# Joining two blocks' exponentials before the ones product in the last group of a decoder layer's self attentions

## The chip, the cores and the metric

The kernel runs on one core of a Trainium2 chip. The core has five engines, each with its own list of instructions: TensorE (PE in the profile; its weight loads are PEld), VectorE (DVE), ScalarE (ACT), GpSimd (POOL) and SyncE (SP), which issues most DMAs. An engine takes its list strictly in order and waits for others by semaphores. The metric is the device time of one execution in microseconds (us), the median of several runs.

## The reference

One decoder layer on `x` (4, 512, 512), with a context of the same shape: x plus a self attention with projections and biases, plus a cross attention without projections, plus a feed-forward part (shared MLP and one expert matrix). 16 heads of 32 columns, all in float32. What matters here is the self attention:

```python
scores = jnp.einsum('bhqd,bhkd->bhqk', q, k) * SCALE
causal = jnp.tril(jnp.ones((Td, Td), dtype=bool))
scores = jnp.where(causal, scores, -jnp.inf)
probs = jax.nn.softmax(scores, axis=-1)
ctx = jnp.einsum('bhqk,bhkd->bhqd', probs, v)
```

## The kernel before

The four batch entries are worked one after the other. For each there is a self attention (class `Attention` with `cross=False`, named `s0` to `s3`), an output projection, a cross attention (`c0` to `c3`), and a feed-forward part whose matmuls fill gaps of the next entry.

**Tiles of an attention.** The 16 heads make four groups `g` of four heads (`HG = 4`). The 512 keys are cut into four blocks `j` of 128. By causality block `j` meets the queries from `j * 128` on, so it has 512, 384, 256 or 128 columns of queries per head. Scores are held transposed (keys on partitions, queries on columns), two heads to a tile of two PSUM banks, four heads in two tiles.

**Three steps of a unit** (`attend`, line 974). A unit is a piece or two of (group, block): for an even group `g` they are `(g,0)`, then `(g,3)` with `(g,1)`, then `(g,2)` with `(g+1,2)`, then `(g+1,0)`, then `(g+1,3)` with `(g+1,1)`. Ten units in all, numbered 0 to 9. `scores` (line 397) writes the scores into PSUM, ScalarE takes their exponentials into SBUF tiles `pt` (line 443), and GpSimd sets the part above the diagonal to zero (line 451, the *mask*). The values of a unit (`values`, line 463) follow two units later: after the scores of unit `n` come the values of unit `n-2`, and at the end those of units 8 and 9 stand behind each other.

**Values** (`shares`, line 470). For each piece, four matmuls (one for each head, each 32 columns of TensorE's array wide, side by side) multiply the exponentials with `v` into the numerators, `pv[:, 0, :]` (line 486 with `u = 0`). The denominators are sums of the exponentials over the keys, made as products with a matrix of ones. For groups 0 to 2 (`added`) VectorE first adds the blocks' exponentials into one tile `sums[g]` (`add_up`, line 551, adds at line 556), and one ones product of 512 columns per head makes the sums (`summed`, line 560, matmul at line 562). For group 3, which is not added, every piece has its own ones product beside its numerators (line 486 with `u = 1`, into `pv[:, 1, :]`), all four accumulated in PSUM.

**The end of a self attention.** The sums of group 2 go to a PSUM pair of their own, `ls`. They are issued with block 0 of group 3 (lines 511 to 513). `spread` and `inverse` (lines 570 and 580) transpose the sums on VectorE, take reciprocals and spread them; `scale` (line 575) multiplies the output of groups 0 to 2 on GpSimd; group 3 is divided on VectorE (line 525). Then `out_projection` (line 739) multiplies the four groups' outputs with `wo`, group by group, with transposes of the context and of the next input between them (lines 255 to 267).

**The cross attentions** already have a joined pair of blocks, in group 1 (`joined = 1`, except in the last): `join` (line 529) adds block 2's exponentials to the second half of block 0's on VectorE, and `joint_sums` (line 539) makes one ones product of the result, placed with block 0, first of its group.

**What sets the order.** The whole body runs under `tc.manual_schedule` for TensorE, VectorE, ScalarE and GpSimd: each engine's instructions stand in the order in which the program calls them. Semaphores follow from what reads and writes which tile. PSUM is four tiles of two banks (`pair`, line 65), which all of the kernel shares. The tiles of `join` have the tag `xin`, two buffers that also hold the next entry's input during its normalization.

Of the kernel before, what the change touches and what calls it, by code (L numbers as in the profile page):

```python
# [26 lines left out]
def decoder_layer(  # L27
# [22 lines left out]
    B, S, D = x.shape  # L50
# [3 lines left out]
    NC = D // P  # L54
# [10 lines left out]
    def pair(name):  # L65

        return ps.tile([P, 2, S], F32, tag="ps", name=name)
# [80 lines left out]
    zero = const.tile([P, 1], F32, name="zero")  # L148
# [121 lines left out]
    class Attention:  # L270
        def __init__(self, q_t, k_t, v, cross, name):
            self.q_t, self.k_t, self.v, self.cross, self.name = q_t, k_t, v, cross, name
            self.nm, self.mrow, self.pv, self.out = {}, {}, {}, None
            self.more, self.sums, self.rden, self.e = {}, {}, {}, None
            self.added = (0, 2) if cross else range(NC - 1)

            self.joined = 1 if cross and name != f"c{B - 1}" else None
            self.joint, self.zero = [], None

        def maxima(self, pieces):  # L280
# [189 lines left out]
        def shares(self, g, blocks):  # L470

            js = {j for j, *_ in blocks}
            first = js == {0} if g % 2 == 0 else js == {2}
            last = js == {2} if g % 2 == 0 else 1 in js
            if first:
                self.pv[g] = pair(f"pv_{self.name}_{g}")
            pv = self.pv[g]
            for u in range(1 if g in self.added else 2):
                if u and g == self.joined and (0 in js or 2 in js):
                    if 0 in js:  # L480
                        self.joint_sums(pv, blocks[0][2])
                    continue
                for n, (j, c, pts) in enumerate(blocks):
                    for r in range(HG):
                        h = g * HG + r
                        nc.tensor.matmul(  # L486
                            pv[r * HD : (r + 1) * HD, u, j * P :],
                            lhsT=ones if u else self.v[:, j, h * HD : (h + 1) * HD],
                            rhs=pts[r // 2][:, r % 2, c : c + S - j * P],
                            start=first,  # L490
                            stop=last and n == len(blocks) - 1,
                            skip_group_check=True,
                        )
            if self.cross:


                if (first if g == 1 else js == {0}) and g - 1 in self.added:
                    self.summed(g - 1, self.pv[g - 1])
                    self.divide(g - 1)
                elif js == {0} and g > 0:  # L500
                    self.scale(g - 1)
                if 1 in js and g == NC - 1:
                    self.scale(g - 1)
                if last and g not in self.added:
                    self.divide(g)
                    if g == NC - 1:
                        self.scale(g)
                return
            if first and g == 0:
                self.out = act.tile([P, NC, S], F32, tag="o_t", name=f"oT_{self.name}")  # L510
            if (first if g in self.added else js == {0}) and g - 1 in self.added:
                self.sum_in = pv if g in self.added else pair(f"ls_{self.name}")
                self.summed(g - 1, self.sum_in)
            if js == {0} and g - 2 in self.added:
                self.scale(g - 2)
            if 1 in js and g - 1 in self.added and g not in self.added:
                self.spread(g - 1, self.sum_in)
                self.scale(g - 1)
            if last and g in self.added:
                nc.scalar.copy(self.out[:, g, :], pv[:, 0, :])  # L520
                if g > 0:
                    self.spread(g - 1, pv)
            elif last:
                num, den = pv[:, 0, :], pv[:, 1, :]
                nc.vector.tensor_tensor(
                    self.out[:, g, :], num, self.inverse(g, den), ALU.mult
                )
# [8 lines left out]
                )  # L536
                self.joint.append(to)

        def joint_sums(self, pv, zero):
            for n in range(2):  # L540
                for r in range(HG):
                    nc.tensor.matmul(
                        pv[r * HD : (r + 1) * HD, 1, n * S // 2 : (n + 1) * S // 2],
                        lhsT=ones,
                        rhs=(self.joint if n else zero)[r // 2][:, r % 2, : S // 2],
                        start=(n == 0),
                        stop=False,
                        skip_group_check=True,
                    )

# [582 lines left out]
```

## Time and profile before

| what | value |
|---|---|
| median of 3 runs | 802.95 us (802.95 to 803.22) |
| profiled execution | 803.28 us |
| its span, first to last instruction | 801.5 us |
| TensorE busy | 794.1 us, 99% of the span |
| VectorE, ScalarE, GpSimd busy | 566.4, 395.4, 340.0 us |
| granted TensorE clock, mean | 1.000 |
| line 486, numerators of self attentions, `pv_s` from `pt_s` and `v`, 128x256 | 385 ns each |
| line 534, joining adds of the cross attentions, 128x512 | 679 ns each |

A row of the page's groups names the line, the engine, the operation, the tile written and the tiles read, the shape, how many there were, the busy time and the mean of one, and then how long the engine sat idle before them and who ended that. A row of a timeline gives the start, the time that a run of like instructions took together, and the same names. Matmuls are pipelined and their ends are modelled, so the distance from one start to the next says more than a duration. A float32 matmul stands as two instructions in the trace, so four heads with one piece are x8. Busy shares are means over the whole span; what one edit is worth has to be read from its own stretch.

### The profile page before, as it was taken

How to read it: one execution, taken by the hardware profiler on the slowest of the kernel's cores; microseconds unless marked ns; L12 is line 12 of the kernel's file. 1: busy time of each engine (PE TensorE's matmuls, PEld its weight loads, DVE VectorE, ACT ScalarE, POOL GpSimd, SP SyncE). 2: the span in 40 equal slices, each digit the busy share in tenths (PEclk: the TensorE clock that was granted, in tenths of full speed). 3: DMA queues.
4: the chain of work that ended last, by engine and by line, in shares of the span. 5: the costliest groups of instructions: out<-in, count | busy, mean ns of one | idle time of the engine just before them, and what ended most of it. 6: DMA issues, size and time to landing. Idle time of an engine off the chain costs nothing.

```text
span 801.5 us, 13955 instructions
## 1 busy us (share of the span) xinstructions
PE 794.1 (99%) x5600; PEld 379.5 (47%) x5600; DVE 566.4 (71%) x963; ACT 395.4 (49%) x450; POOL 340.0 (42%) x523
## 2 busy tenths in 40 slices
PE   8999999999999999999999999999999999999998
PEld 7444554445444454444544445444444454444444
DVE  2478866888678854588867786688859766988512
ACT  2557426871547515666045752687056824674110
POOL 3435612664234732267233482266423653475100
PEclk9999999999999999999999999999999999999999
DMA  9700000001000000021100000000102000000101
GB/s 311 266 28 1 2 1 1 2 28 54 1 27 1 2 1 0 2 80 53 53 14 14 1 2 1 0 1 2 54 28 80 2 2 0 1 2 2 52 1 52
DMA packets 16337, 24.51 MB, mean 31 GB/s; under 512 B 2064, under 2 KB 6416, under 8 KB 16272
## 3 DMA queue, kind: packets, MB, share of 16 engines
q1 hardware_dynamic: 15552, 22.96, 8.3%
q8 instruction: 44, 0.72, 0.4%
q10 hardware_dynamic: 720, 0.66, 0.2%
q14 instruction: 21, 0.17, 0.1%
HBM read 19.42 MB, written 4.19 MB: 29 GB/s over the span
## 4 chain that ended last, share of the span: by engine, by line
PE 96%; ACT 2%; issue 1%; DVE 0%; POOL 0%; POOLq 0%
PE pm_qk L245 13%; PE pm_d L233 7%; PE pm_u L245 7%; PE pm_v L233 7%; PE pm_o L745 7%; PE pm_e L233 7%; PE pv_c L486 6%; PE pv_s L486 6%; PE sm_c L297 6%; PE sm_s L297 6%; PE sc_s L409 5%; PE sc_c L409 5%; PE sc_s L420 1%; PE sc_c L420 1%; PE pv_s L562 1%
## 5 line engine op out<-in xcount | busy, mean ns | idle before, releaser
L328 DVE TENSOR_REDUCE nm_s<-s_s 128x2 f32<-128x1024 f32 (+3 forms) x128 | 96.9, 810 | 31.0 <-POOL s_s L316 30.9
L328 DVE TENSOR_REDUCE nm_c<-s_c 128x2 f32<-128x1024 f32 (+3 forms) x128 | 95.9, 811 | 31.0 <-POOL s_c L316 31.0
L308 ACT COPY s_s<-sm_s 128x1024 f32<-128x1024 f32 x80 | 77.1, 1015 | 70.7 <-PE sm_s L297 36.4
L308 ACT COPY s_c<-sm_c 128x1024 f32<-128x1024 f32 x80 | 77.1, 1016 | 35.9 <-PE sm_c L297 16.2
L316 POOL TENSOR_SCALAR_AFFINE_SELECT s_c<-s_c 128x512 f32<-128x512 f32 (+1 forms) x80 | 44.1, 552 | 100.2 <-ACT s_c L308 100.2
L316 POOL TENSOR_SCALAR_AFFINE_SELECT s_s<-s_s 128x512 f32<-128x512 f32 (+1 forms) x80 | 44.0, 554 | 92.9 <-ACT s_s L308 92.9
L556 DVE TENSOR_TENSOR sum_s<-sum_s,pt_s 128x256 f32<-128x256 f32 (+2 forms) x72 | 60.0, 898 | 15.4 <-PE pv_s L486 15.4
L443 ACT ACTIVATE pt_c<-sc_c 128x1024 f32<-128x1024 f32 x64 | 61.7, 1031 | 18.4 <-PE sc_c L420 10.1
L233 PE MATMUL pm_d<-wdown_sb,hT 128*128 128x512 f32 x128 | 61.5, 610 | 0.0
L451 POOL TENSOR_SCALAR_AFFINE_SELECT pt_c<-pt_c 128x512 f32<-128x512 f32 (+1 forms) x64 | 52.5, 828 | 21.1 <-ACT pt_c L443 20.7
L245 PE MATMUL pm_u<-fT,wup_sb 128*128 128x512 f32 x128 | 59.3, 604 | 0.0
L443 ACT ACTIVATE pt_s<-sc_s 128x1024 f32<-128x1024 f32 x56 | 53.9, 1029 | 10.5 <-POOL pt_s L451 5.5
L233 PE MATMUL pm_v<-wv_sb,xnT 128*128 128x512 f32 x128 | 58.8, 600 | 0.0
L745 PE MATMUL pm_o<-wo_sb,oT_s 128*128 128x512 f32 x128 | 57.8, 596 | 0.0
L409 PE MATMUL sc_c<-cqT,ckT 32*128 32x384 f32 (+3 forms) x512 | 56.4, 464 | 0.9 <-ACT sum_c L443 0.9
L245 PE MATMUL pm_qk<-xnT,wk_sb 128*128 128x512 f32 x120 | 57.3, 607 | 0.0
L245 PE MATMUL pm_qk<-xnT,wq_sb 128*128 128x512 f32 x120 | 56.7, 604 | 0.0
L233 PE MATMUL pm_e<-wexp_sb,fT 128*128 128x512 f32 x120 | 56.3, 604 | 0.0
L451 POOL TENSOR_SCALAR_AFFINE_SELECT pt_s<-pt_s 128x512 f32<-128x512 f32 (+1 forms) x56 | 48.0, 867 | 16.8 <-ACT pt_s L443 16.2
L409 PE MATMUL sc_s<-qT,kT 32*128 32x128 f32 (+3 forms) x512 | 54.0, 464 | 0.9 <-ACT sum_s L443 0.9
L297 PE MATMUL sm_c<-ckT,cqT 32*128 32x512 f32 (+3 forms) x512 | 47.5, 460 | 0.0
L297 PE MATMUL sm_s<-kT,qT 32*128 32x512 f32 (+3 forms) x512 | 47.0, 461 | 0.0
(177 smaller groups left out, 1274.8 us busy)
## 6 DMA issues: line engine op xcount, KB each, us to landing
cv<-in_ctx_dram SPq DMA_DIRECT2D x16, 256.0 KB, 3.7
out_dram<-x SPq DMA_DIRECT2D x15, 256.0 KB, 2.1
xin<-in_x_dram SPq DMA_DIRECT2D x12, 256.0 KB, 2.6
x<-in_x_dram SPq DMA_DIRECT2D x12, 256.0 KB, 4.0
wv_sb<-in_wv_dram SPq DMA_DIRECT2D x1, 1024.0 KB, 8.3
wo_sb<-in_wo_dram SPq DMA_DIRECT2D x1, 1024.0 KB, 9.9
wup_sb<-in_wup_dram SPq DMA_DIRECT2D x1, 1024.0 KB, 9.9
wdown_sb<-in_wdown_dram SPq DMA_DIRECT2D x1, 1024.0 KB, 12.1
```

Of the source, the lines that this page charges most:

```text
L233: nc.tensor.matmul(pm, lhsT=lhs_t[:, c, t * P : (t + 1) * P], rhs=w[:, c, :], start=(c == 0), stop=(c == NC - 1),)
L245: nc.tensor.matmul(pm, lhsT=w[:, c, f * P : (f + 1) * P], rhs=rhs_t[:, c, :], start=(c == 0), stop=(c == NC - 1),)
L297: nc.tensor.matmul(scs[r // 2][:, r % 2, c : c + (i + 1) * P], lhsT=self.q_t[h, g, i * P : (i + 1) * P], rhs=self.k_t[h, g, : (i + 1) * P] ...
L308: nc.scalar.copy(s, scs[n])
L316: nc.gpsimd.affine_select(out=diagonal, in_=diagonal, compare_op=ALU.is_ge, fill=NEG, base=0, pattern=[[0, 2], [0, len(pieces)], [-1, P]], ...
L328: nc.vector.tensor_reduce(self.nm[g][:, i, 2 * n : 2 * n + 2], made[n][:, :, c : c + (i + 1) * P], axis=AX.X, op=ALU.max, negate=True,)
L409: nc.tensor.matmul(scs[r // 2][:, r % 2, c : c + S - j * P], lhsT=self.k_t[h, g, j * P : (j + 1) * P], rhs=self.q_t[h, g, j * P :], start= ...
L443: nc.scalar.activation(pt, scs[n], AF.Exp)
L451: nc.gpsimd.affine_select(out=diagonal, in_=diagonal, compare_op=ALU.is_ge, fill=0.0, base=0, pattern=[[0, 2], [0, len(pieces)], [1, P]], ...
L486: nc.tensor.matmul(pv[r * HD : (r + 1) * HD, u, j * P :], lhsT=ones if u else self.v[:, j, h * HD : (h + 1) * HD], rhs=pts[r // 2][:, r % ...
L556: nc.vector.tensor_tensor(to, to, pts[n][:, :, c : c + S - j * P], ALU.add)
L745: nc.tensor.matmul(pms[t // 2][:, t % 2, :], lhsT=a.out[:, c, t * P : (t + 1) * P], rhs=wo_sb[:, c, :], start=(c == 0), stop=(c == NC - 1),)
```

## The change

In the self attentions block 2 of group 3 is joined with block 0, as it is in the cross attentions' group 1, and the products are put in a new order. Three things happen.

1. `joined` becomes group 3 (`NC - 1`) for self attentions. The separate ones products of block 2 (256 columns a head) and of block 0 (512 columns) go. `attend` now calls `join` for this group: two adds on VectorE, 128x512 elements each, behind the adds of group 2's last block.
2. The ones products of group 3 are all made with its last unit, in this order: those of blocks 3 and 1 (the first of which starts the accumulation), then `joint_sums` with two runs of 256 columns a head: block 0's first half, and the joined half.
3. The sums of group 2 (`summed`, into `ls`) are issued behind the numerators of blocks 3 and 1, ahead of group 3's ones products, and no longer behind block 0's products.

So the end of TensorE's list in a self attention reads: numerators of block 2, of block 0, of blocks 3 and 1; sums of group 2; ones of blocks 3 and 1; joint ones. In the cross attentions `joint_sums` gets the flag `first`, and its order is what it was.

```diff
-            self.joined = 1 if cross and name != f"c{B - 1}" else None
+            self.joined = NC - 1 if not cross else 1 if name != f"c{B - 1}" else None
...
             for u in range(1 if g in self.added else 2):
                 if u and g == self.joined and (0 in js or 2 in js):
                     if 0 in js:
-                        self.joint_sums(pv, blocks[0][2])
+                        self.zero = blocks[0][2]
+                    if 0 in js and self.cross:
+                        self.joint_sums(pv, self.zero, first=True)
                     continue
+                joining = u and g == self.joined and not self.cross
                 for n, (j, c, pts) in enumerate(blocks):
                     for r in range(HG):
...
-                            start=first,
-                            stop=last and n == len(blocks) - 1,
+                            start=n == 0 if joining else first,
+                            stop=last and n == len(blocks) - 1 and not joining,
                             skip_group_check=True,
                         )
+                if joining:
+                    self.joint_sums(pv, self.zero, last=True)
+                elif g == self.joined and not self.cross and 1 in js:
+                    self.sum_in = pair(f"ls_{self.name}")
+                    self.summed(g - 1, self.sum_in)
...
-            if (first if g in self.added else js == {0}) and g - 1 in self.added:
-                self.sum_in = pv if g in self.added else pair(f"ls_{self.name}")
+            if first and g > 0 and g in self.added:
+                self.sum_in = pv
                 self.summed(g - 1, self.sum_in)
...
-        def joint_sums(self, pv, zero):
+        def joint_sums(self, pv, zero, first=False, last=False):
             for n in range(2):
                 for r in range(HG):
...
-                        start=(n == 0),
-                        stop=False,
+                        start=first and n == 0,
+                        stop=last and n == 1,
```

## The prediction

> **What bounds the kernel now.** I read the page first. Two of its lines say where a microsecond counts:
>
> ```profile
> span 801.5 us, 13955 instructions
> PE 794.1 (99%) x5600; PEld 379.5 (47%) x5600; DVE 566.4 (71%) x963; ACT 395.4 (49%) x450; POOL 340.0 (42%) x523
> ...
> PE 96%; ACT 2%; issue 1%; DVE 0%; POOL 0%; POOLq 0%
> ```
>
> TensorE is busy in 99% of the span and makes 96% of the chain that ended last. So whatever lengthens or shortens TensorE's own row of work, a stall included, goes into the time at full size, and what the other engines do counts only where TensorE waits for it. Next I read the timeline of TensorE at the end of the first self attention (line 486 with v: numerators; with ones, and line 562: denominators; line 745: output projection):
>
> ```profile
> 88.86 1.07 PE L486 MATMUL pv_s<-pt_s,v 128*32 128x256 f32 x16
> 89.75 0.61 PE L486 MATMUL pv_s<-pt_s,ones 128*32 128x256 f32 x8
> 90.18 1.04 PE L486 MATMUL pv_s<-pt_s,v 128*32 128x512 f32 x8
> 91.04 1.04 PE L486 MATMUL pv_s<-pt_s,ones 128*32 128x512 f32 x8
> 91.90 1.04 PE L562 MATMUL ls_s<-sum_s,ones 128*32 128x512 f32 x8
> 92.76 1.05 PE L486 MATMUL pv_s<-pt_s,v 128*32 128x128 f32 x16
> 93.62 1.05 PE L486 MATMUL pv_s<-pt_s,ones 128*32 128x128 f32 x16
> 94.60 3.70 PE L745 MATMUL pm_o<-wo_sb,oT_s 128*128 128x512 f32 x8
> ```
>
> The durations include a modelled tail, so I take prices from one start to the next. I call the eight rows N7 (block 2 of groups 2 and 3), O7 (ones on block 2), N8 and O8 (block 0), S (the sums of group 2), N9 and O9 (blocks 3 and 1), and the projection. N7 takes 0.89 us, O7 0.43, N8, O8, S and N9 0.86 each, O9 0.98 with the change to line 745. Nothing waits here. The same eight rows stand at 272.12, 469.09 and 642.88 us with the same spacing to 0.02 us, so one working serves four times.
>
> Then I read who feeds N9, in the timelines of ScalarE, GpSimd and VectorE:
>
> ```profile
> 88.88 1.94 ACT L443 ACTIVATE pt_s<-sc_s 128x1024 f32<-128x1024 f32 x2 [0.43 <-PE sc_s L420]
> ...
> 89.97 0.83 POOL L451 TENSOR_SCALAR_AFFINE_SELECT pt_s<-pt_s 128x512 f32<-128x512 f32 x1 [0.21 <-ACT pt_s L443]
> 90.88 0.96 POOL L451 TENSOR_SCALAR_AFFINE_SELECT pt_s<-pt_s 128x512 f32<-128x512 f32 x1
> ...
> 90.22 1.12 DVE L556 TENSOR_TENSOR sum_s<-sum_s,pt_s 128x512 f32<-128x512 f32 x1
> 91.33 0.72 DVE L583 STREAM_TRANSPOSE dt_s<-pv_s 128x512 f32<-128x512 f32 x1
> ```
>
> The exponentials of blocks 3 and 1 start when their scores leave TensorE and end at 90.82. GpSimd's two masks of them end at 90.80 and 91.84. N9 multiplies just these tiles, two heads from each, and it starts at 92.76: 0.92 us of slack. The slack is 0.92, 0.92 and 0.94 in the other three attentions (masks ending at 275.10, 472.07 and 645.83).
>
> **The change part by part.** Order before: N7 O7 N8 O8 S N9 O9. Order after: N7 N8 N9 S O9 J, where J is the joint product, two runs of 256 columns.
>
> *Removed and moved products.* Ones columns per head fall from 1280 to 1024 (O7 256 and O8 512 go, J brings 512). J has 16 instructions and 512 columns, as O8 and O9 have in columns: 0.86 us. The row of TensorE work becomes 0.43 us shorter per attention, 1.7 us in all. That is what the change would give if nothing waited.
>
> *N9 moves ahead.* What stood between N8 and N9, O8 and S (1.72 us), and O7 ahead of them (0.43 us) were its cover. After the change N8 runs from 89.75 to 90.61, and N9 wants to start at 90.61. Its first two heads wait for the first mask (90.80), its third for the second (91.84). TensorE works in its written order, so S, O9 and J queue behind N9 and cannot fill the gap. How soon does TensorE start after a release? At 156.58 two exponentials take 1.96 us, to 158.54, and the scores waiting for them start at 158.59: 0.05 us. So N9's third head starts at 91.89, and as its first two heads' short piece alone is done by then, which spares next to nothing of four heads side by side, N9 ends at 91.89 + 0.86 = 92.75. Then S, O9 and J: 3 x 0.86, to 95.34, and 0.11 to the projection: 95.45 against 94.60. **Sum per attention: +0.86 us**: a stall of 1.28 us less 0.43 removed.
>
> The mask's end is the term that decides, so I bound it. It asked at 90.88; the same form alone takes 0.64 us (line 316, 128x512, mean 641 ns). Undisturbed it ends at 91.52: +0.54 us. Here it took 0.96 and ended 0.50 after the VectorE add beside it (91.34). That add began 0.58 before the first mask ended and finished 0.54 after it, so the two engines' instructions with SBUF operands take turns. After the change a joining add stands behind the last add, where a PSUM transpose stood; if it took the turn ahead of the mask, that would be one add later, 0.54 us: +1.40. I keep 91.84: the masks from 87.6 on end at 88.67, 89.76, 90.80 and 91.84, the adds between them at 89.48, 90.30 and 91.34, so turns alternate, and the mask has been waiting since 90.88.
>
> The Trainium skill has a rule that speaks against the change here (SBUF — State Buffer, "SBUF: two separate sides"): a VectorE instruction with two SBUF inputs and a GpSimd instruction that reads SBUF hold one shared pair of ports exclusively, whole instruction by whole instruction. The rows above agree with it. It does not say who comes next when both wait, so by the rule alone the sum could be +0.86 or +1.40 per attention; by the rows it is +0.86.
>
> *Two joining adds on VectorE*, 128x512 each. The same form in the cross attentions (line 534) took 1.28 us for two; beside GpSimd an add of this size took up to 0.96 from start to start. So 1.2 to 1.9 us on a VectorE that is behind: busy without a gap from 85.62 to 97.28. They delay the reciprocals of groups 1, 2 and 3 and the last multiplication, to 99.2 at worst. Who waits? J's second half at 94.9 needs the adds (done by 93.3). GpSimd's scalings of groups 1 and 2, now done at 94.44 and 96.25, are needed by the projection at 99.88 and 104.19. The tightest is the transposes of the next input at 99.01, which need the PSUM pair that the last multiplication frees: 97.28 now, 98.6 to 99.2 after, when TensorE comes to them at 99.87. Cost: nothing, with 0.7 us left; were the cover gone, each further 0.1 us would cost 0.1 us in three attentions.
>
> *S later.* Its inputs are complete at 91.34; it moves from 91.90 to 92.75 and is not held. Its PSUM pair is the same and needed by nobody else. Group 2's reciprocal waits for VectorE anyway (94.7). *N8 earlier* by 0.43: its masks end at 89.76, it comes at 89.75: at most 0.1 us, swallowed by the wait that follows. No DMA is issued, moved or passed: the joined tiles use input buffers that were last read long before (66.84), and SP's queue is unchanged. Cross attentions keep their order.
>
> **Sum.** 4 x 0.86 = 3.4 us on the profiled execution's 803.28 us (span 801.5 and 1.8 around it): 806.7. It lies 0.3 above the median of the runs shown, so I predict 802.95 + 3.43 = **806.4 us**. Everything later on TensorE shifts as it stands, since it waits for nothing long enough to absorb a shift.
>
> **Rivals.**
> 1. *The mask is quicker, undisturbed*: 4 x 0.54, 805.1. For: VectorE's adds could shift. Against: they keep their place. Chance 0.08.
> 2. *A joining add goes ahead of the mask*: 4 x 1.40, 808.6. For: it is queued directly behind the add that holds the mask up. Against: alternation. Chance 0.10.
> 3. *Faster: N9 finds its masks done*, and the 0.43 us count in full: 802.95 - 1.7 = 801.2. This decides from a mask end of 90.56 or sooner; break-even is 90.99. For it speaks only that GpSimd has idle time in this stretch. Against: the second exponential itself ends at 90.82, and the quickest mask takes 0.64. Chance 0.05.
> 4. *The change does not do what it says*: the written order does not become TensorE's, S stays ahead of N9. S is then held to 91.34 by VectorE's add (its last two heads), N9 ends at about 93.1, O9 and J at 94.8: +0.35 each at most, and about 0 if S's early heads run ahead: 803 to 804.4. Against: the trace of before follows the written order everywhere in this stretch. Chance 0.03.
> 5. *VectorE's delay reaches the projection* on top of the forecast (PSUM pair later than 99.87): above 808.6. Chance 0.04.
>
> The forecast itself has 0.70 (805.8 to 807.1, for 0.1 us either way at each restart). The range takes in rivals 1 and 2: 805.0 to 808.6, with 0.88 inside. A measurement here can tell about 0.2%, 1.6 us, from no change. Faster by more: 0.05 (rival 3). Within: 0.03 (rival 4). Slower by more: 0.92 (the forecast and rivals 1, 2 and 5).
>
> **What would show it.** Right: in the timeline N9 follows N8 directly, its start spread out, with weight loads waiting for POOL pt_s L451 about 1.1 us four times; the projection's first row comes 6.6 us after N7's start, against 5.74 now; the chain of waits goes through L451. The second mask ends 2.98 us after N7's start. Wrong: this distance is 5.3 us (rival 3), or the second mask ends at 3.5 us (rival 2), or the transposes behind the projection's first rows wait for VectorE (rival 5).

## The result, and the profile after

The changed kernel takes 806.49 us, median of 5 runs (806.39 to 806.74), beside 802.96 us for the kernel before: ratio 1.0044, interval 1.0032 to 1.0055. It is slower by 3.5 us; 806.4 was forecast, 805.0 to 808.6 the range. The profiled execution took 806.74 us.

First the page of the changed kernel:

```profile
span 805.0 us, 13955 instructions
PE 795.1 (99%) x5600; PEld 382.7 (48%) x5600; DVE 571.7 (71%) x971; ACT 395.3 (49%) x450; POOL 339.5 (42%) x523
...
PE 92%; ACT 3%; POOL 2%; issue 2%; DVE 0%; POOLq 0%
```

The span is 3.5 us longer, and TensorE has as many instructions as before (5600, with fewer columns). Its share of the chain that ended last fell from 96% to 92%; GpSimd and ScalarE took over. Where this happens is in TensorE's timeline at the end of the first self attention (in this file line 489 is numerators and ones, 570 the sums of group 2, 550 the joint product, 753 the projection):

```profile
88.97 2.40 PE L489 MATMUL pv_s<-pt_s,v 128*32 128x256 f32 x28
92.00 1.06 PE L489 MATMUL pv_s<-pt_s,v 128*32 128x128 f32 x12 [0.62 <-POOL pt_s L451]
92.68 1.23 PE L570 MATMUL ls_s<-sum_s,ones 128*32 128x512 f32 x8
93.54 1.24 PE L489 MATMUL pv_s<-pt_s,ones 128*32 128x128 f32 x16
94.41 0.81 PE L550 MATMUL pv_s<-pt_s,ones 128*32 128x256 f32 x8
94.84 0.81 PE L550 MATMUL pv_s<-jn_s,ones 128*32 128x256 f32 x8
95.57 3.70 PE L753 MATMUL pm_o<-wo_sb,oT_s 128*128 128x512 f32 x8
```

The first row holds 28 instructions: N7, N8 and the four of N9 that belong to its first two heads' short piece. Then nothing starts until 92.00, when N9's third head gets its tile; the bracket names GpSimd's mask. S, O9 and J follow without a gap, and the projection starts 6.60 us after N7. GpSimd and VectorE in the same stretch:

```profile
90.99 0.96 POOL L451 TENSOR_SCALAR_AFFINE_SELECT pt_s<-pt_s 128x512 f32<-128x512 f32 x1
...
90.34 1.11 DVE L564 TENSOR_TENSOR sum_s<-sum_s,pt_s 128x512 f32<-128x512 f32 x1
91.38 1.12 DVE L542 TENSOR_TENSOR jn_s<-pt_s,pt_s 128x512 f32<-128x512 f32 x1
```

The second mask ends at 91.95, 2.98 us after N7's start as before, and N9's third head starts 0.05 later. The joining add, issued at 91.38, did not go ahead of the mask: it ended at 92.49, 0.54 after it. The chain that ended last runs through just these instructions:

```profile
89.90 1.03 ACT pt_s L443
90.93 0.06 issue
90.99 0.97 POOL pt_s L451
91.96 0.04 issue
92.00 1.06 PE pv_s L489 x10
```

I use one measure for all kernels below: the distance from N7's first matmul to the projection's first. It was 5.73 us in each of the four attentions before (5.74 by the rounded starts of the rows); now it is 6.60, 6.60, 6.60 and 6.58. The excess, summed before rounding, adds up to 3.45 of the 3.53 us between the medians.

### The profile page after: what moved, and what is told of

The parts are those of the page before. It is cut to its first block, busy times and chain, and to the rows that moved or that the text cites. A ratio compares the mean times of both kernels' runs of the same rounds, so it can differ in the third digit from the quotient of the medians.

```text
span 805.0 us, 13955 instructions
## 1 busy us (share of the span) xinstructions
PE 795.1 (99%) x5600; PEld 382.7 (48%) x5600; DVE 571.7 (71%) x971; ACT 395.3 (49%) x450; POOL 339.5 (42%) x523
## 4 chain that ended last, share of the span: by engine, by line
PE 92%; ACT 3%; POOL 2%; issue 2%; DVE 0%; POOLq 0%
PE pm_qk L245 13%; PE pm_d L233 7%; PE pm_u L245 7%; PE pm_v L233 7%; PE pm_o L753 7%; PE pm_e L233 7%; PE pv_c L489 6%; PE sm_c L297 6%; PE sm_s L297 5%; PE sc_c L409 5%; PE sc_s L409 4%; PE pv_s L489 4%; POOL pt_s L451 2%; PE sc_c L420 1%; ACT pt_s L443 1%
```

## The experiments

**Theory A**: N9 waits for GpSimd's second mask because its cover was taken away, and all that stands behind N9 on TensorE queues up; the wait costs more than the removed products save. **Theory B**: the two joining adds on a VectorE that is already late, or denominators that come late because J stands last, cost the time; N9's place does not.

| kernel | distances, us | 4 excesses, sum | median, us | kernel before beside it | ratio, interval |
|---|---|---|---|---|---|
| before | 5.73 5.73 5.73 5.73 | 0 | 802.96 | | |
| changed | 6.60 6.60 6.60 6.58 | +3.45 | 806.49 | 802.96 | 1.0044, 1.0032 to 1.0055 |
| e1_sums_back | 6.11 6.11 6.10 6.09 | +1.47 | 804.56 | 803.01 | 1.0020, 1.0011 to 1.0029 |
| e2_order_alone | 6.60 6.60 6.60 6.58 | +3.45 | 806.50 | 803.01 | 1.0044, 1.0031 to 1.0056 |
| e3_no_last_masks | 5.58 5.58 5.58 5.58 | -0.63 | 802.91 | 803.01 | 0.9998, 0.9989 to 1.0007 |
| e4_no_join_adds | 6.60 6.60 6.60 6.58 | +3.45 | 806.50 | 803.01 | 1.0043, 1.0029 to 1.0057 |
| e5_half_ahead | 5.68 5.67 5.67 5.66 | -0.25 | 802.74 | 803.17 | 0.9995, 0.9986 to 1.0005 |
| e6_adds_sooner | 5.31 5.31 5.31 5.31 | -1.71 | 801.35 | 803.17 | 0.9978, 0.9969 to 0.9987 |
| e7_adds_alone | 5.73 5.73 5.73 5.73 | 0 | 803.25 | 803.17 | 1.0000, 0.9991 to 1.0009 |
| e8_masks_elsewhere | 5.58 5.58 5.58 5.58 | -0.63 | 802.50 | 803.14 | 0.9992, 0.9983 to 1.0001 |
| e9_sooner_alone | 6.41 6.41 6.41 6.41 | +2.70 | 805.76 | 803.14 | 1.0034, 1.0021 to 1.0046 |

**Order alone (e2_order_alone).** The kernel before, with all its products; only the end of TensorE's list is reordered:

```diff
+            alone = g == NC - 1 and not self.cross
+            if alone and 0 in js:
+                self.later = blocks
             for u in range(1 if g in self.added else 2):
+                if u and alone and 0 in js:
+                    continue
+                if u and alone and 1 in js:
+                    self.sum_in = pair(f"ls_{self.name}")
+                    self.summed(g - 1, self.sum_in)
+                    blocks = self.later + blocks
```

> The kernel before with its own products (block 2's ones product O7 stays, nothing is joined), only in the order N7 O7 N8 N9 S O8 O9. Theory A: N9 would like to start at 91.04 and its third head is held to 91.89 as in the changed kernel; behind the wait stand N9, S, O8 and O9, 4 x 0.86, as many as there (N9, S, O9, J). So the time is that of the changed kernel although 0.43 us more of products are made in each attention: 6.60 us from N7 to the projection, 806.4 us. Theory B: no joining adds and no J, so no loss: 803.0 us.

It took 806.50 us. Its timeline, from N7 on:

```profile
88.65 1.07 PE L495 MATMUL pv_s<-pt_s,v 128*32 128x256 f32 x16
89.53 0.61 PE L495 MATMUL pv_s<-pt_s,ones 128*32 128x256 f32 x8
89.97 1.25 PE L495 MATMUL pv_s<-pt_s,v 128*32 128x512 f32 x12
91.68 1.06 PE L495 MATMUL pv_s<-pt_s,v 128*32 128x128 f32 x12 [0.47 <-POOL pt_s L451]
92.36 1.23 PE L571 MATMUL ls_s<-sum_s,ones 128*32 128x512 f32 x8
93.22 2.10 PE L495 MATMUL pv_s<-pt_s,ones 128*32 128x512 f32 x24
95.25 3.70 PE L754 MATMUL pm_o<-wo_sb,oT_s 128*128 128x512 f32 x8
```

O7 is there and N8 starts 0.43 later after N7 than in the changed kernel, but N9's third head starts at the same distance (91.68 - 88.65 = 3.03, as 92.00 - 88.97), and four products stand behind the wait. The whole loss comes with the order. The products that the change removes were removed from a wait, and nothing was gained by it. One half of theory B falls: here are no joining adds and no J. Its other half does not fall here, since O8 and O9, the denominators, stand as late as J does; the runs without the last masks, below, keep J last and lose nothing.

**Joining adds alone, and left out (e7_adds_alone, e4_no_join_adds).** The first adds the two joining adds to the kernel before; nothing reads them. The second takes them out of the changed kernel.

```diff
+                if not a.cross and waiting[0][0][1] == 2 and waiting[0][1][0] == NC - 1:
+                    a.join(waiting[0][1], waiting[1][0])
```

> The kernel before, with the two joining adds of the self attentions made on VectorE and read by nothing. Theory A: hidden on VectorE, TensorE's list untouched: 803.0 us. If the first of them took GpSimd's turn, the second mask would end 0.54 later, at 92.38, still ahead of N9 at 92.76. Theory B: 804 to 806.5 us.

```diff
             (g, _, c, pts), pts0 = two, zero[3]
+            if not self.cross:
+                self.joint = [p[:, :, S // 2 :] for p in pts0]
+                return
```

> The changed kernel without the two joining adds on VectorE in the self attentions; J's second half is made of block 0's exponentials alone, so block 2 is left out of the sums of group 3. TensorE's list is the same. Theory A: the adds are hidden and the mask's end is set by the adds before them: 806.5 us, 6.60 us from N7 to the projection, VectorE's last multiplication about 1.6 us sooner. Theory B: the adds cost the time: 803 to 804 us.

The adds alone cost nothing that shows (ratio 1.0000, every distance 5.73); leaving them out gives nothing back (806.50, 6.60). In e7 the mask beside the first joining add ends at 92.14, 2.98 us after N7's start (89.16):

```profile
91.17 0.96 POOL L451 TENSOR_SCALAR_AFFINE_SELECT pt_s<-pt_s 128x512 f32<-128x512 f32 x1
```

VectorE's last multiplication ends 9.77 us after N7's start in the changed kernel and 9.26 without the adds, a shift that shows nowhere in TensorE's distances. About 1.6 us had been expected; it is 0.51, for without the adds VectorE waits 0.85 us for S, which takes up most of the difference.

**No last masks (e3_no_last_masks), and the masks elsewhere (e8_masks_elsewhere).**

```diff
                     diagonal = pt[:, :, : 2 * P].rearrange("p u (k q) -> p u k q", k=2)
+                if (g, j) == (NC - 1, NT - 1) and not self.cross:
+                    pts.append(pt)
+                    continue
```

> The changed kernel without GpSimd's two masks of blocks 3 and 1 of group 3 in the self attentions; these two blocks' exponentials above the diagonal are therefore counted in, in numerators and sums. Theory A: N9 then waits for the second exponential (90.82 in the first attention) alone: its third head starts at 90.87, and N9, S, O9, J and 0.12 end at 94.43, against 94.60 before: -0.17 us in each attention, 802.3 us. Theory B: VectorE's work is all there, so the loss stays: 806.5 us, or somewhat less as VectorE's adds are less disturbed.

The distance is 5.58, as expected: the mask is what N9 waits for, and behind it the second exponential, which ends at 90.69; N9's third head starts 0.05 after it:

```profile
89.67 1.02 ACT L443 ACTIVATE pt_s<-sc_s 128x1024 f32<-128x1024 f32 x1
90.74 0.85 PE L492 MATMUL pv_s<-pt_s,v 128*32 128x128 f32 x10
```

VectorE's joining adds and the late J are all there, and the loss is gone: this is where the rest of theory B falls. But the time is 802.91, and the attentions' -0.63 should have given 802.4. The trace has the rest behind the last matmul: from its start to the end of the span it is 4.05 us against 3.62 before. Two closing instructions of GpSimd stand 0.32 us apart there, against 0.03 before, and one of them is 0.14 longer. So I gave GpSimd two tiny masks on a tile of their own in place of the two that were taken out (VectorE sets this tile once, at the start of the kernel):

```diff
+                    nc.gpsimd.affine_select(
+                        out=tiny, in_=tiny, compare_op=ALU.is_ge, fill=0.0,
+                        base=0, pattern=[[0, 2]], channel_multiplier=1,
+                    )
```

> As the run without the last masks (blocks 3 and 1 of group 3 are not masked in the self attentions, so what lies above their diagonal is counted in), but GpSimd makes a mask of 128x2 elements on a tile of its own in place of each of them, so that its list is as long as in the changed kernel. Nothing on TensorE waits for these. The attentions should take what they took there, 5.575 us from N7 to the projection. There the time was 802.9, some 0.5 us above what the attentions explain, and 0.43 us of this lay behind the last matmul, where GpSimd's closing instructions stood apart. If that gap comes from where GpSimd's list ends, it is gone here, and the time is 802.3 to 802.4; if it comes from the missing masks themselves, 802.9.

802.50 us, distance 5.58, and 3.63 us behind the last matmul. With GpSimd's list as long as in the changed kernel the gap is gone. That the length of the list makes it is not shown beyond these two kernels, and why the closing instructions stood apart stays open.

**The sums back (e1_sums_back).** S behind N8 again, all else as changed.

```diff
-                elif g == self.joined and not self.cross and 1 in js:
+                elif g == self.joined and not self.cross and 0 in js:
```

> Theory A (the wait of the last numerators N9 for GpSimd's second mask sets the loss; everything behind N9 on TensorE queues up): with S, the sums of group 2, back behind block 0's numerators N8 and everything else as in the changed kernel, S stands in the gap. S itself is held for its last two heads by VectorE's last add (91.34 in the first attention), so its third head starts at 91.39, and S, N9, O9 and J follow, 4 x 0.86: the projection comes 6.09 us after N7's start instead of 6.60 (5.74 before), +0.35 us in each of four attentions: 804.4 us. Theory B (the two joining adds on VectorE, or the denominators that come late because J stands last, cost the time; N9's place does not): 806.5, as in the changed kernel.

804.56 us and 6.11: S waits for VectorE's last add instead. The waits of the weight loads in the first attention name it:

```profile
PEld ls_s L570 <- DVE sum_s L564: 0.7, 1, 0.7
```

Each attention is 0.35 to 0.38 us longer than in the kernel before. So the change took away two covers, one for the mask and one for the adds, and putting S back helps only as far as S itself is ready.

**A half of J ahead (e5_half_ahead), and the adds sooner (e6_adds_sooner).** The half of J that needs block 0 alone, and then S, go behind N8:

```diff
                     if 0 in js and self.cross:
                         self.joint_sums(pv, self.zero, first=True)
+                    elif 0 in js:
+                        self.joint_sums(pv, self.zero, first=True, halves=(0,))
+                        self.sum_in = pair(f"ls_{self.name}")
+                        self.summed(g - 1, self.sum_in)
                     continue
...
                 if joining:
-                    self.joint_sums(pv, self.zero, last=True)
-                elif g == self.joined and not self.cross and 1 in js:
-                    self.sum_in = pair(f"ls_{self.name}")
-                    self.summed(g - 1, self.sum_in)
+                    self.joint_sums(pv, self.zero, last=True, halves=(1,))
```

> The changed kernel's products in the order N7 N8 J0 S N9 O9 J1, J0 being the half of the joint product that needs block 0 alone (0.43 us). Theory A: J0 fills the gap to 91.04, S's third head waits for VectorE's last add (91.39), and S, N9, O9 (0.86 each) and J1 (0.43) follow: 5.66 us from N7 to the projection, 0.08 less than before: 802.6 us. N9 no longer waits for a mask. Theory B: the joining adds and a last joint product are still there: about 806.

802.74 us, distance 5.67: a tie with the kernel before, though each attention has 0.43 us less to do; S's third head still waits for VectorE:

```profile
PEld ls_s L571 <- DVE sum_s L565: 0.2, 1, 0.2
```

e6 takes this wait away too. `inverse` is cut in two, `turned` (the transpose out of PSUM, made where it was) and `inverted` (reciprocal and second transpose, made behind the last adds), for group 0:

```diff
+                if g == 1:
+                    self.rden[0] = self.turned(0, pv[:, 1, :])
-                if g > 0:
+                elif g > 0:
                     self.spread(g - 1, pv)
...
-            if js == {0} and g - 2 in self.added:
-                self.scale(g - 2)
+            if js == {0} and g == NC - 1:
+                self.scale(0)
+                self.scale(1)
...
+                    if not a.cross:
+                        a.inverted(0, a.rden[0])
                     a.join(waiting[0][1], waiting[1][0])
```

> The order of the run with J0 ahead, and VectorE's reciprocal and second transpose for group 0 (0.96 us), with GpSimd's scaling of group 0, put off behind the last adds of group 2. Theory A: VectorE's adds then end at about 90.4, so S finds its sums at 91.04; with less VectorE beside it the second mask ends by 91.7, so N9 finds its tiles at 91.90. Nothing on TensorE waits, and the whole 0.43 us of removed products counts: 5.31 us from N7 to the projection, 801.2 us. If VectorE's last multiplication (about 98.9) then holds the transposes of the next input (98.6), 0.1 to 0.3 us come back in three attentions: up to 802.1. Theory B: 806.

801.35 us, ratio 0.9978 (0.9969 to 0.9987): faster than both kernels. VectorE and GpSimd, and TensorE from N7 on:

```profile
87.79 1.72 DVE L568 TENSOR_TENSOR sum_s<-sum_s,pt_s 128x512 f32<-128x512 f32 x2
89.44 0.24 DVE L605 RECIPROCAL rden_s<-dt_s 128x16 f32<-128x16 f32 x1
...
90.35 0.77 DVE L546 TENSOR_TENSOR jn_s<-pt_s,pt_s 128x512 f32<-128x512 f32 x1
...
90.85 0.76 POOL L451 TENSOR_SCALAR_AFFINE_SELECT pt_s<-pt_s 128x512 f32<-128x512 f32 x1 [0.28 <-ACT pt_s L443]
```

```profile
88.83 1.93 PE L493 MATMUL pv_s<-pt_s,v 128*32 128x256 f32 x24
90.58 0.61 PE L554 MATMUL pv_s<-pt_s,ones 128*32 128x256 f32 x8
91.01 1.04 PE L574 MATMUL ls_s<-sum_s,ones 128*32 128x512 f32 x8
91.87 1.05 PE L493 MATMUL pv_s<-pt_s,v 128*32 128x128 f32 x16
92.73 1.05 PE L493 MATMUL pv_s<-pt_s,ones 128*32 128x128 f32 x16
93.59 0.61 PE L554 MATMUL pv_s<-jn_s,ones 128*32 128x256 f32 x8
94.14 3.70 PE L764 MATMUL pm_o<-wo_sb,oT_s 128*128 128x512 f32 x8
```

The last add of group 2 ends at 89.51, well ahead of S at 91.01. The mask ends 0.50 us after the end of the add ahead of it, as in the changed kernel; but this add is now the first joining one, and it has ended by 91.11, 0.20 sooner after N7. So the mask ends at 91.61, ahead of N9 at 91.87. Every row stands at its own length behind the one before, and the distance, 5.31, is that of before less the 0.43 us of O7. VectorE's last multiplication ends at 97.80, ahead of the transposes at 98.55, so nothing comes back. Of all these kernels this alone gets the full worth of the removed products.

**The adds sooner, in the changed order (e9_sooner_alone).** The same edits of `inverse`, `shares` and `attend`, with N9 ahead of S and all of J last.

> The changed kernel's order on TensorE (N9 ahead of S), with VectorE's reciprocal of group 0 put off behind the last adds, as in the fastest version. Theory A: N9's wait follows the end of the second mask, which came 2.78 us after N7's start there, against 2.98 in the changed kernel. So 0.20 us less in each attention: 6.40 us from N7 to the projection, 805.7 us. If VectorE's busy row were what costs the time (theory B), the adds ending 1 us sooner would bring more, down to 803.

805.76 us and 6.41. The second mask (0.77 us from 90.69) ends 2.78 us after N7's start (88.67), and N9 follows it:

```profile
90.69 0.77 POOL L451 TENSOR_SCALAR_AFFINE_SELECT pt_s<-pt_s 128x512 f32<-128x512 f32 x1 [0.28 <-ACT pt_s L443]
...
91.51 1.06 PE L489 MATMUL pv_s<-pt_s,v 128*32 128x128 f32 x12 [0.63 <-POOL pt_s L451]
```

The mask came 0.19 sooner and the distance is 0.19 shorter; the last add came 1.8 us sooner (it ends 0.70 us after N7's start, against 2.48). The time follows the mask and not VectorE's row.

## Why the prediction was right, point by point

- *N9 loses its cover and waits for the second mask*: right, and shown by the order alone (e2) and by the masks left out (e3, e8). The mask's end at 2.98 us after N7, the restart 0.05 us after it, and the order of the turns held in the trace. +0.86 per attention was forecast, 0.85 to 0.87 measured.
- *The removed products are worth 0.43 us per attention*: right as a length of work (e6: 5.73 to 5.31). In the changed kernel it is worth nothing: e2, which keeps them, takes the same time. The sum of the prediction, a stall of 1.28 less 0.43, says the same in other words, since a shorter list ahead of N9 lengthens the stall by as much.
- *The joining adds are hidden*: right (e4, e7). They ended at 93.09 in the profile of the changed kernel, 1.7 us after the first was issued and inside 1.2 to 1.9 us, and the PSUM pair was free at 98.74, 1.24 us ahead of the transposes at 99.98 (0.7 was the worst case). The prediction's 0.96 us from start to start as the most for one such add was too low: its own rows have 1.11 (90.22 to 91.33), and the first joining add took 1.04.
- *A joining add ahead of the mask* (rival 2): did not happen, in the changed kernel or in e7. The rule of the Trainium skill that was weighed there (SBUF — State Buffer, "SBUF: two separate sides") names the exclusive pair of ports; the rows say what it leaves open, who comes next. The mask, waiting since 90.99, came before an add issued at 91.38.
- *The quicker mask* (rival 1): did not happen; this mask took 0.96 us again. In e6 it took 0.76, because the add ahead of it had ended 0.20 sooner.
- *Faster* (rival 3) was priced rightly at its end: with no wait left, e6 gains 1.7 us over four attentions. Its condition cannot be met in this order, as the prediction's argument against it said: even without masks (e3) the exponential holds N9, and 0.16 of the 0.43 us per attention is left.
- *S stays ahead of N9* (rival 4): did not happen, the rows follow the new order. e1 has the order of this rival, and there each attention took 0.35 to 0.38 us more, where this rival had 0.35 at most.
- *Weight loads waiting about 1.1 us*: the longest is 0.9, and TensorE's own row shows 0.62, since the profile counts idle time from the modelled ends of the matmuls. The distance between starts was the sign to look at, 6.60 as forecast.
- N9 itself took 0.68 us from its third head to S, not 0.86, since its first two heads had run ahead. The 0.18 us comes back at the end, where the later heads are still at work: 1.16 us from J to the projection, against 0.98 from O9 to it before. The sum was not touched.

## What to carry to other kernels

In a list that one engine takes in order, work that stands between a producer's start and its consumer is cover. Before a consumer is moved forward, subtract the moved time from its slack (here 0.92 us of slack, 2.15 us of cover moved or removed). Removed work pays in full only where the engine has nothing to wait for behind it; so first make the producers ready (here VectorE's adds), then shorten the list.

## What the runs showed of the hardware that was not expected

- After a wait in the middle of four side by side products the heads stay out of step: in the changed kernel N9's third and fourth heads stand beside the next piece of the first two, and the rows behind still start 0.86 us apart, though each takes longer (S 1.23 us, 1.04 before).
- TensorE's starts are not strictly in the written order. In e1 N9's first heads start at 91.25, before S's last at 91.64, as if each head kept an order of its own (not tested). A head that waits for another engine did hold all that stood behind it, though: in the changed kernel no matmul starts between 91.10 and 92.00.
- The same VectorE add of 128x512 elements, the last one of group 2, took 1.11 us in the changed kernel and 0.68 in e3, which has no mask there. So the 0.43 us more are not more work; they come with the masks. In the changed kernel the add ended 0.54 us after the mask that was under way when it was issued.

```profile
90.10 0.68 DVE L567 TENSOR_TENSOR sum_s<-sum_s,pt_s 128x512 f32<-128x512 f32 x1
```

- Two GpSimd instructions fewer in each self attention left 0.43 us more behind the last matmul (e3), and two tiny ones took it away again (e8).
